# Cross-attention with a column-normalised softmax: a fused row minimum, a first batch by whole products, a last output in pieces, and new tables of order

## The chip, the cores and the metric

The kernel runs on one NeuronCore of a Trainium2 chip. The metric is the device time of one execution in microseconds (us), lower is better. The core has five engines that run side by side, each in its own program order: TensorE (PE in the profile, its weight loads PEld), VectorE (DVE), ScalarE (ACT), GpSimd (POOL) and SyncE (SP), which issues transfers. Matrix products are written to PSUM, eight banks of 512 fp32 columns on 128 partitions; everything else lies in SBUF.

## The reference

For each of 32 batches `x` and `y` (the input `ctx_2048`) are 256 x 1024 in fp32, and the three weights are 256 x 256.

```
x_q = (w_qk y)^T            x_k = w_qk x            x_v = w_v x + b_v
energy = x_q x_k                                      # 1024 x 1024
attention = softmax over the last axis of energy
attention = attention / (1e-7 + sum of attention over its rows)     # each column is normalised
x_r = x_v attention                                   # 256 x 1024
out = x + relu(w_t (x - x_r) + b_t)
```

## The kernel before

Algebra first. With G = w_qk^T w_qk, energy = y^T (G x), so each batch makes "keys" G x once and multiplies by y. The value path is folded: w_t w_v x is made directly ("values", `V`), and w_t x + b_t is made beside it (`x` products, `xP`). Energies carry a minus sign, so that a row **minimum** is what the softmax subtracts, and exp runs with scale -1.

Precision: each fp32 operand is split into a HIGH part and a LOW part of a faster fp32 form, and a product is three matmuls (HIGH HIGH, HIGH LOW, LOW HIGH, `ORDER`). A 2 x 2 block product is made by Winograd's scheme with seven block products instead of eight: `chain` (L278) makes the words P1 to P7 on three banks `a`, `b`, `c`; partial results are read out of `a` by ACT (`r1`, `r2`, `r3`) and added back by DVE (`c11`, `c22`, `c12`). Keys (`k`), energies (`E0` to `E3`) and x products (`x`) all go this way. So each `P` word is three matmuls of 512 columns on PE.

Energies are made in four pairs of row tiles, `E0` to `E3`. Tile n has 128 rows and 1024 columns and fills two banks: odd tiles banks 2 and 3 (`a` and `d`), even tiles banks 0 and 1 (`b` and `c`). The next pair's P1 writes bank `a` again, so it must wait until the odd tile of the pair before is read. The work of a tile is:

- the row minimum. Three of a pair's four blocks get theirs with the sum that makes them (`energy_block`, L451, on DVE with a running minimum). The fourth, the block `21` in bank `a`, is finished by PE itself, and `energy_least` (L463, the word `m21`) takes its minimum;
- `exp` on ACT with the minimum as bias and the row sum as second output, `ri` (reciprocal, DVE), `h` (ACT, exp times reciprocal, HIGH), `sum` (DVE, column sums into `acc`), `l` (DVE, LOW), for each half of 512 columns;
- `A n c h`: the attention product, three matmuls into one of banks 4 to 7.

After the last tile come `cols`, `inv`, `turn` (column sums, their inverse, spread over the partitions), `div` (DVE, banks 4 to 7 times the inverse into `z`), `join` (POOL, plus the x product), `pos` (ACT, relu), `add` (POOL, a transfer that adds x from memory) and `st` (SP, the store).

The order of everything is written out by hand in three tables of words, `FIRST`, `STEADY` and `LAST` (L575, L609, L629). A word with `+` belongs to the next batch, with `-` to the one before. Each engine gets its words in the order of the table and works them strictly in that order. The weights are prepared ahead of `FIRST`, in straight code: G, its seven left blocks in two parts (`left_blocks`, L173), w_t turned, w_v times w_t.

Of the kernel before, what the change touches and what calls it, by code (L numbers as in the profile page):

```python
# [17 lines left out]
def kernel(  # L18
# [142 lines left out]
    def gram(into, w):  # L161
        for k in range(KC):
            matmul(into[:, 0, :C], w[:, k, :P], w[:, k], k == 0, k == KC - 1)
            matmul(into[:, 1, P:C], w[:, k, P:], w[:, k, P:], k == 0, k == KC - 1)

    def square(into, left, right):
        for i in range(KC):
            for k in range(KC):
                matmul(
                    into[:, i, :C], left[:, k, ts(i, P)], right[:, k], k == 0, k == KC - 1  # L170
                )

    def left_blocks(name, to, w, engine):  # L173

        s = sums[name][:, 0].rearrange("p (s c) -> p s c", s=4)
        a11, a12, a21, a22 = (w[:, k, ts(i, P)] for i in range(2) for k in range(2))
        s1, s2, s3, s4 = (s[:, j] for j in range(4))
        engine.tensor_tensor(s1, a21, a22, ALU.add)
        engine.tensor_tensor(s3, a21, a11, ALU.subtract)
        engine.tensor_tensor(s2, s1, a11, ALU.subtract)  # L180
        engine.tensor_tensor(s4, a12, s2, ALU.subtract)
        act.copy(to[:, HIGH, 0:2], w[:, :, :P])
        act.copy(to[:, HIGH, 2], a22)
        act.copy(to[:, HIGH, 3:], s)
        engine.tensor_tensor(to[:, LOW, 0:2], w[:, :, :P], value(to[:, HIGH, 0:2]), ALU.subtract)
        engine.tensor_tensor(to[:, LOW, 2], a22, value(to[:, HIGH, 2]), ALU.subtract)
        engine.tensor_tensor(to[:, LOW, 3:], s, value(to[:, HIGH, 3:]), ALU.subtract)
# [384 lines left out]

    FIRST = """  # L575
        ldx0 ldx1 xT1 xh0 xl0 xT2 xh1 xl1 xT4 xTh1 xT3 xTl1 xTh0 xTl0 V00 V11 kP1 ldy0 kr1
        kP6 V10 kP5 ldy1 yh11 kr2 yh01 ys01 kP2 kP7 kr3 ys03 yh00 kc22 kc11 V01 kP3 kP4
        yl01 ys02 khD yl00 kc12 kT1 ys04 klD kh21 vh1 vh0 ysh0 kT3 vl1 kT2 kT4 kTh0 kl21
        kTh1 vl0 E0P2 +ldx0 ysl0 kTl1 xP1 E0P1 xP2 xP5 E0r1 yh10 xr1 E0P6 xP6 kTl0 E0r2
        +xh0 E0P7 E0c11 xc11 E0P5 E0r3 E0P4 E0c22 E0P3 E0m21 E0c12 exp1 +xT1 ys11 ys12 ri1  # L580
        sum10 ys14 h10 h11 l10 exp0 E1P1 E1r1 l11 A100 ri0 sum11 h01 +xl0 yl10 sum01 E1P6
        l01 E1r2 A111 sum00 E1P7 E1P5 yl11 h00 ys13 l00 E1r3 E1c22 E1P4 E1m21 xr2 E1P2
        +ldx1 ysh1 E1c11 E1P3 +xT3 E1c12 xP7 ysl1 exp3 ri3 sum30 xr3 h30 h31 exp2 l30 A000
        A011 xP4 xc22 l31 ri2 E2P1 xP3 E2r1 A311 sum31 E2P6 xc12 A101 h21 h20 E2r2 +xh1
        l21 E2P7 sum21 +xT2 sum20 l20 E2r3 xw21 E2P5 +ldy0 E2P4 E2c22 +yh01 +xTh0 E2m21
        E2P2 E2c11 E2P3 A110 A001 E2c12 exp5 ri5 sum50 +xl1 A211 A300 A301 h50 l50 exp4
        E3P1 h51 +xT4 E3r1 A010 ri4 +yh00 E3P6 sum51 A310 h41 E3r2 h40 E3P7 l51 sum41 l41
        sum40 E3r3 l40 E3P5 +xTh1 E3P4 E3c22 E3P2 A201 E3m21 +ldy1 E3P3 E3c11 +ys01 A200
        A210 exp7 A511 E3c12 +ys03 +yl01 ri7 h70 sum70 A510 +yh10 exp6 l70 +xTl0 +kP1
        +xTl1 sum71 ri6 +ys11 +yl00 +kr1 A501 +kP6 A410 h61 sum61 l61 +kr2 sum60 +kP7 h71  # L590
        +ys02 +ys13 +ys12 h60 l60 +ys04 +kP5 +kr3 A401 +kc22 +kP2 +ys14 l71 +kP3 +ysh0
        +kP4 +kc11 +khD +ysl0 +kc12 +kT1 +kh21 cols +kT2 +kl21 A710 +kT4 A701 A610 +kT3
        A500 A411 +klD A400 A711 +kTh1 +E0P1 +kTh0 +E0r1 inv turn +kTl1 A601 +kTl0 A700
        A611 +E0P6 A600 +E0P2 +E0r2 +yh11 +E0P7 div1 +E0P5 +E0r3 div0 ++ldx0 +E0P4 +ysh1
        +E0c22 +E0m21 +V10 +E0c11 +exp1 +ri1 +h10 +E0P3 +E0c12 +l10 +sum10 +exp0 +V11 +V01
        +ri0 +vh1 +E1P1 +h00 +sum11 +E1r1 +h11 +V00 +sum00 +h01 +E1P6 +vl1 +xP1 +l00 +E1r2
        +yl11 join0 +E1P7 +l11 +E1P2 +vh0 +l01 +E1r3 +sum01 +E1P5 +E1P4 +vl0 +E1c22 +xP2
        +xr1 pos0 ++xh0 join1 +ysl1 +xP6 +yl10 +E1P3 +E1m21 +E1c11 +E1c12 +exp3 ++ldx1
        +xP5 +A111 +xr2 +xP7 +ri3 +h30 +exp2 +xc11 +sum30 +xr3 +A100 +l30 +ri2 ++xT3 +A000
        +h20 +E2P1 +A300 +xP4 +sum31 ++xl0 +h21 +E2r1 +E2P6 +h31 +E2r2 ++xT1 +sum20 pos1  # L600
        +xc22 +l20 +l21 +xP3 +sum21 +E2P7 +xc12 +E2r3 ++xT2 +E2P5 +E2P4 ++ldy0 +l31 +E2P2
        +xw21 ++xh1 +E2c22 ++ys01 +E2P3 ++xT4 ++xTh0 +E2m21 +A110 +E2c11 +A101 +A010 +exp5
        +A011 +E2c12 +ri5 +sum50 +h50 +l50 +exp4 +A001 +ri4 +E3P1 +h40 ++xTl0 ++xl1 add1
        +E3r1 ++ys02 +h41 +h51 ++ldy1 +A200 +sum40 +A301 +l40 +E3P6 +l41 +sum51 +sum41
        +A311 +E3P2 +l51 ++ys04 ++yh00 +E3r2 ++ys03 +E3P7 ++yh01 +E3r3 +E3P5 ++xTh1 ++ys11
        +E3c11 st1 +A211 ++ysh0 +E3c22 +E3P4 +A310 +E3m21 +E3P3 ++yh11 +exp7 +E3c12 +ri7
        +sum70 +A500 +A210 +h70 +l70 +exp6 +A201 +A510 +sum71 +ri6 +h60 ++kP1
    """
    STEADY = """  # L609
        +xTl1 +yl01 +ys13 sum61 A400 A511 +kr1 h61 +kP6 +ysl0 +ys12 sum60 l60 +kr2 +kP2  # L610
        l61 +kP7 +kP5 A700 -add0 +yl00 +ys14 h71 +kr3 +kP4 cols +kc11 +kc22 +kP3 l71 A600
        +kc12 +khD +kT1 +kT3 A410 A501 A411 A710 A401 +kTh0 +kh21 +ysh1 +klD +kT2 +kTl0
        inv +kT4 +kl21 turn A711 A610 +kTh1 A611 A701 +E0P1 +E0P2 +E0r1 +kTl1 +yl11 +E0P6
        A601 +E0r2 +E0P7 -st0 +E0P5 div1 +E0c11 div0 +E0r3 +yh10 +E0c22 +E0P4 +E0P3 +E0m21
        +V10 +yl10 +V11 +E0c12 join1 +exp1 +ri1 +exp0 +V00 +h10 +sum10 +sum11 +ri0 +l10
# [62 lines left out]
```

## Time and profile before

| | |
|---|---|
| median of 3 runs | 2215.44 us (2185.95 to 2217.18) |
| the profiled execution | 2221.73 us, span of its instructions 2219.9 us |
| mean granted TensorE clock | 0.959 |
| busy PE / DVE / ACT / POOL | 1978.3 / 1718.9 / 1431.0 / 1401.6 us (89 / 77 / 64 / 63%) |
| transfers | 136.76 MB, mean 62 GB/s |

The profile is one execution. The span runs from the first to the last instruction, and the profiled execution's time is 1.8 us more. Engines overlap, so their busy times don't add. A row of a group of instructions gives the busy time and, behind it, the idle time of that engine just before them with what ended it. In the timeline a row's first number is the start, the second how long it took, and a bracket holds the idle time before it. Nearly all instructions are recorded under L62, a helper that keeps the order, so rows are told apart by tile names: `banks` is PSUM, `efs` the exponentials' HIGH and LOW parts, `small` the per-row numbers, `acc` the column sums, `rs` the read-out blocks, `gf` keys, `yd` and `ysum` the parts of y, `xf` those of x, `uf` and `vws` values, `gws` and `tws` the left blocks of weights, `z` and `xe` the output and the x product. The fused sum with a running minimum is CUSTOM_DVE_ANT_0 in the profile, followed by a DVE_READ_ACCUMULATOR2_ANT that delivers the minimum.

### The profile page before, as it was taken

How to read it: one execution, taken by the hardware profiler on the slowest of the kernel's cores; microseconds unless marked ns; L12 is line 12 of the kernel's file. 1: busy time of each engine (PE TensorE's matmuls, PEld its weight loads, DVE VectorE, ACT ScalarE, POOL GpSimd, SP SyncE). 2: the span in 40 equal slices, each digit the busy share in tenths (PEclk: the TensorE clock that was granted, in tenths of full speed). 3: DMA queues.
4: the chain of work that ended last, by engine and by line, in shares of the span. 5: the costliest groups of instructions: out<-in, count | busy, mean ns of one | idle time of the engine just before them, and what ended most of it. 6: DMA issues, size and time to landing. Idle time of an engine off the chain costs nothing. (4 is left out here: it accounts for less than half of the span.)

```text
span 2219.9 us, 25140 instructions
## 1 busy us (share of the span) xinstructions
PE 1978.3 (89%) x8671; PEld 1552.5 (70%) x8671; DVE 1718.9 (77%) x3049; ACT 1431.0 (64%) x2227; POOL 1401.6 (63%) x974
## 2 busy tenths in 40 slices
PE   6898989889898889898899988898989998988986
PEld 4677777777777777676777766776777777767775
DVE  2787877778778787777787777877877877878875
ACT  4676666766667666666666666666766666666663
POOL 7476666566666656766667656567667667566661
PEclk8999999999999999999999999999999999999998
DMA  1112212212122122122221221212221212212213
GB/s 64 39 49 76 67 48 67 76 48 67 48 76 67 48 76 60 55 67 57 68 67 48 76 67 48 76 49 65 67 76 49 75 49 68 67 51 74 67 29 76
DMA packets 46432, 136.76 MB, mean 62 GB/s; under 512 B 4448, under 2 KB 5344, under 8 KB 46304
## 3 DMA queue, kind: packets, MB, share of 16 engines
q1 hardware_dynamic: 36672, 101.20, 12.8%
q0 software_dynamic: 9216, 33.56, 9.1%
q8 instruction: 68, 1.11, 0.2%
q14 instruction: 60, 0.49, 0.1%
q10 hardware_dynamic: 416, 0.39, 0.1%
HBM read 101.58 MB, written 33.55 MB: 61 GB/s over the span
## 5 line engine op out<-in xcount | busy, mean ns | idle before, releaser
L62 PE MATMUL banks<-efs,uf 128*128 128x512 f32 x3072 | 801.6, 401 | 1.3 <-DVE efs L62 1.3
L62 PEld LDWEIGHTS banks<-efs,uf 128*128 128x128 f32 x3072 | 597.4, 195 | 134.1 <-DVE efs L62 2.2
L62 PE MATMUL banks<-gf,yd 128*128 128x512 f32 x1152 | 347.5, 421 | 184.3 <-ACT efs L62 144.7
L62 ACT COPY rs<-banks 128x512 f32<-128x512 f32 x480 | 283.0, 590 | 265.4 <-PE banks L62 264.9
L62 DVE SCALAR_TENSOR_TENSOR acc<-banks,small,acc 128x512 f32<-128x512 f32 x448 | 334.8, 747 | 142.7 <-ACT efs L62 139.3
L62 PE MATMUL banks<-gf,ysum 128*128 128x512 f32 x1536 | 442.6, 407 | 1.5 <-DVE acc L62 0.3
L62 ACT ACTIVATE banks<-banks,small 128x1024 f32<-128x1024 f32 x256 | 278.0, 1086 | 246.9 <-DVE small L62 246.8
L62 ACT ACTIVATE efs<-banks,small 128x512 fp32r<-128x512 f32 x512 | 350.0, 692 | 114.0 <-DVE small L62 108.0
L62 PEld LDWEIGHTS banks<-gf,yd 128*128 128x128 f32 x1152 | 210.8, 195 | 278.4 <-ACT efs L62 83.0
L62 DVE SCALAR_TENSOR_TENSOR efs<-banks,small,efs 128x512 fp32r<-128x512 f32 x512 | 369.7, 743 | 17.3 <-ACT efs L62 17.2
L62 PEld LDWEIGHTS banks<-gf,ysum 128*128 128x128 f32 x1536 | 283.9, 193 | 110.3 <-ACT rs L62 42.5
L62 POOL TENSOR_TENSOR gf<-sums,gf 128x1024 fp32r<-128x1024 f32 x96 | 229.4, 2404 | 177.5 <-ACT gf L62 177.5
L62 POOL TENSOR_TENSOR sums<-raws 128x256 f32<-128x256 f32 (+1 forms) x192 | 185.2, 966 | 159.6 <-DMA raws<-in_ctx_dram 152.0
L62 POOL TENSOR_TENSOR xf<-raws,xf 128x1024 fp32r<-128x1024 f32 x64 | 153.4, 2397 | 175.2 <-ACT xf L62 166.0
L62 POOL TENSOR_TENSOR xf<-sums,xf 128x1024 fp32r<-128x1024 f32 x64 | 153.1, 2394 | 156.4 <-ACT xf L62 156.4
L62 PEld LDWEIGHTS banks<-vws,xf 128*128 128x128 f32 x1536 | 210.4, 206 | 19.8 <-ACT xf L62 8.5
L62 PE MATMUL banks<-vws,xf 128*128 128x256 f32 x1536 | 211.1, 297 | 10.9 <-ACT xf L62 7.5
L62 DVE CUSTOM_DVE_ANT_0 banks<-banks,rs 128x512 f32<-128x512 f32 x256 | 176.5, 694 | 48.5 <-PE banks L62 35.5
L62 PE MATMUL banks<-xf,gws 128*128 128x512 f32 x672 | 180.6, 405 | 21.7 <-ACT yd L62 14.5
L62 PE MATMUL banks<-xf,tws 128*128 128x512 f32 x672 | 190.6, 392 | 3.0 <-ACT rs L62 2.9
L62 POOL TENSOR_TENSOR yd<-raws,yd 128x512 fp32r<-128x512 f32 (+1 forms) x128 | 138.1, 1079 | 70.8 <-ACT yd L62 70.7
L62 PEld LDWEIGHTS banks<-xf,gws 128*128 128x128 f32 x672 | 118.7, 188 | 72.7 <-ACT banks L62 30.9
(76 smaller groups left out, 2380.7 us busy)
## 6 DMA issues: line engine op xcount, KB each, us to landing
raws<-in_x_dram SPq DMA_DIRECT2D x64, 512.0 KB, 4.2
raws<-in_ctx_dram SPq DMA_DIRECT2D x64, 512.0 KB, 4.0
z<-in_x_dram POOLq DMA_DIRECT2D x64, 512.0 KB, 5.3
out_dram<-z SPq DMA_DIRECT2D x64, 512.0 KB, 3.2
z<-in_L_xattn_w_t_dram ACTq DMA_DIRECT2D x1, 256.0 KB, 4.8
z<-in_L_xattn_w_v_dram SPq DMA_DIRECT2D x1, 256.0 KB, 5.9
z<-in_L_xattn_w_qk_dram ACTq DMA_DIRECT2D x1, 128.0 KB, 2.7
z<-in_L_xattn_w_qk_dram SPq DMA_DIRECT2D x1, 128.0 KB, 2.5
```

Of the source, the lines that this page charges most:

```text
L62: self.last = getattr(self.engine, name)(*args, **kwargs)
```

## The change

Four parts.

1. `energy_least` is one fused instruction instead of two: it adds zeros to the block in bank `a`, writes it back in place, and takes the running minimum from `mB`.
2. The first batch does without Winograd's scheme for its keys (`first_keys`, 24 matmuls for 21), its x products (`first_x`, 24 for 21) and its first pair of tiles (`first_energy`, 24 for 21). So the weights' seven left blocks aren't needed at the start; their making (words `G...` and `T...`) goes into `FIRST` and moves to POOL. x's HIGH and LOW parts of the first batch are partly made on DVE (`Fxh0`, `Fxl0`, `Fxl1`). y's first half is loaded at the start.
3. The last batch's output isn't divided, joined, rectified, added to by a transfer and stored by 1024 columns, but in halves: with relu(d + e) + x written as max(d, -e) + (x + e), `Zs` makes x + e and `Zn` -e ahead of time, and after the last attention products there remain `Zd` (divide in place, in PSUM), `Zm` (maximum), `Za` (sum) and `Zt` (store).
4. `FIRST`, `STEADY` and `LAST` are new tables; `STEADY` now begins at `E0P1`, and the last two batches are in `LAST`.

```diff
     def energy_least(b, p):
-        dve.tensor_reduce(small["mD", b, p], eb["a"], AX.X, ALU.min)
-        dve.tensor_tensor(small["m1", b, p], small["mD", b, p], small["mB", b, p], ALU.min)
+        dve.tensor_tensor_reduce(
+            out=eb["a"],
+            in0=eb["a"],
+            in1=zeros_row,
+            scale=1.0,
+            scalar=small["mB", b, p],
+            op0=ALU.add,
+            op1=ALU.min,
+            accum_out=small["m1", b, p],
+        )
...
+    zeros_row = nc.const_aps.tensor(0.0, [P, MB], F32)
...
+    def first_keys(j, m, k):
+        for i in range(KC):
+            for h in range(MH):
+                matmul(
+                    (kb["b"], kb["c"], kb["a"], banks[:, 3])[2 * i + h],
+                    gt[:, j, k, ts(i, P)],
+                    xf[:, m, 2 * k + h],
+                    (j, m, k) == (HIGH, HIGH, 0),
+                    (j, m, k) == (LOW, HIGH, 1),
+                )
+    def whole(into, left, right):
+        for j, m in ORDER:
+            for k in range(KC):
+                matmul(
+                    into, left(j, k), right(m, k),
+                    (j, m) == ORDER[0] and k == 0, (j, m) == ORDER[-1] and k == KC - 1,
+                )
...
+    def xl_dve(k):
+        at = slice(2 * k, 2 * k + 2)
+        dve.tensor_tensor(
+            flat(xf[:, LOW, at]), raws["x", 0, k], flat(value(xf[:, HIGH, at])), ALU.subtract
+        )
...
+    def first_least(b, n):
+        dve.tensor_reduce(small[f"m{n}", b, 0], flat(tile_banks(n)), AX.X, ALU.min)
...
+    def out_divided(b, c, h):
+        p = pair(2 + c)[:, h]
+        dve.scalar_tensor_tensor(p, p, ubias[:, c], rc[:, ts(h, MB)], ALU.add, ALU.mult)
+    def out_max(b, c, h, kept):
+        p = pair(2 + c)[:, h]
+        dve.tensor_tensor(p if kept else z[:, c, ts(h, MB)], p, xe[:, c, ts(h, MB)], ALU.max)
+    def out_add(b, c, h, kept):
+        zh, o = z[:, c, ts(h, MB)], raws["o", b, c][:, ts(h, MB)]
+        if kept:
+            dve.tensor_tensor(zh, pair(2 + c)[:, h], o, ALU.add)
+        else:
+            pool.tensor_tensor(zh, zh, o, ALU.add)
...
     STEADY = """
-        +xTl1 +yl01 +ys13 sum61 A400 A511 +kr1 h61 +kP6 +ysl0 +ys12 sum60 l60 +kr2 +kP2
...
+        E0P1 -cols ysh1 kTh1 -inv --st0 kTl1 -A610 -A601 -A711 E0r1 kTh0 -turn E0P6 -div0
...
-    for b in range(1, B - 1):
+    for b in range(1, B - 2):
         do(STEADY, b)
```

How the tables move instructions, at three places.

DVE, where a batch's first energy pair begins, in every steady batch. Before, from the turned inverse (STREAM_TRANSPOSE, `turn`) on: the second row is `div1`, the next two `E0c11`, then `div0`, `E0c22`, `E0m21` (two rows) and `E0c12`. ISA is the fused sum and, on 128x1, its accumulator's read.

```order
L62 STREAM_TRANSPOSE acc<-sc 128x1024
L62 SCALAR_TENSOR_TENSOR z<-banks,ubias,acc 128x1024
L62 ISA banks,small<-banks,rs 128x512
L62 ISA small 128x1
L62 SCALAR_TENSOR_TENSOR z<-banks,ubias,acc 128x1024
L62 ISA banks,small<-banks,rs 128x512
L62 ISA small 128x1
L62 TENSOR_REDUCE small<-banks 128x1
L62 TENSOR_TENSOR small<-small 128x1
L62 ISA banks,small<-banks,rs,small 128x512
```

The same place on DVE in the changed kernel: `turn`, `div0` and `div1`, `E0c22`, the new `E0m21`, `E0c11`, `ri1`, `E0c12`.

```order
L62 STREAM_TRANSPOSE acc<-sc 128x1024
L62 SCALAR_TENSOR_TENSOR z<-banks,ubias,acc 128x1024 x2
L62 ISA banks,small<-banks,rs 128x512
L62 ISA small 128x1
L62 ISA banks,small<-banks,const-float32-0.0,small 128x512
L62 ISA small 128x1
L62 ISA banks,small<-banks,rs 128x512
L62 ISA small 128x1
L62 RECIPROCAL small<-small 128x1
L62 ISA banks,small<-banks,rs,small 128x512
```

Both divisions now stand ahead of `E0c22`, `E0c11` stands behind the minimum, and the reciprocal of the odd tile stands ahead of `E0c12`.

PE in the same batch, from the third pair's last products to the fourth pair's first. Before, from `E2P4 E2P2` (two words, six matmuls on `gf,yd`): three attention words, `E2P3`, one attention word, then `E3P1`.

```order
L62 MATMUL banks<-gf,yd 128x512 x6
L62 MATMUL banks<-efs,uf 128x512 x9
L62 MATMUL banks<-gf,ysum 128x512 x3
L62 MATMUL banks<-efs,uf 128x512 x3
L62 MATMUL banks<-gf,yd 128x512 x3
```

In the changed kernel, from `E2P4` on: `E2P3`, five attention words, `E3P1`.

```order
L62 MATMUL banks<-gf,yd 128x512 x3
L62 MATMUL banks<-gf,ysum 128x512 x3
L62 MATMUL banks<-efs,uf 128x512 x15
L62 MATMUL banks<-gf,yd 128x512 x3
L62 MATMUL banks<-efs,uf 128x512 x6
```

Between the product that finishes the odd tile's block (`E2P4`) and the one that overwrites its bank (`E3P1`) stood six words, `E2P2` among them; `E2P2` has moved ahead, and there stand six.

PE at the start of the program. With - the values' and keys' products of before, with + those of the changed kernel: the turned w_t (`z`, 128x128), G's corner, w_v times w_t (128x256), the 24 key products and the 48 value products.

```order
-L62 MATMUL banks<-xe,z 128x256 x4
-L62 MATMUL banks<-vws,xf 128x256 x24
-L62 MATMUL banks<-xf,gws 128x512 x6
-L62 MATMUL banks<-vws,xf 128x256 x12
+L62 MATMUL banks<-z 128x128 x5
+L62 MATMUL banks<-z,rs 128x128
+L62 MATMUL banks<-z 128x256 x4
+L62 MATMUL banks<-xf,efs 128x512 x24
+L62 MATMUL banks<-vws,xf 128x256 x48
```

The keys now stand ahead of all values, and read x's two parts alone, not the sums of x's blocks that POOL makes.

More of the change, by code (lines that the diff above doesn't have):

```diff
@@ L159, in load_y, with word, once @@
         )
[L161 to L187, printed above, removed]
+    words = {}
+    def word(name, do, *args):
+        words[name] = lambda b: do(b, *args)
+    def once(name, do, *args, **more):
+        words[name] = lambda b: do(*args, **more)
     for k, start in enumerate((load, act.dma_start)):
@@ L571 @@
         word(f"st{c}", stored, c)
-    FIRST = """
[L576 to L607, printed above, removed]
@@ L608 @@
     """
     STEADY = """
-        +xTl1 +yl01 +ys13 sum61 A400 A511 +kr1 h61 +kP6 +ysl0 +ys12 sum60 l60 +kr2 +kP2
[L611 to L615, printed above, removed]
@@ new lines @@
+        E0r2 E0P2 --st1 +ldx0 -A611 kTl0 E0P7 -div1 E0r3 E0P5 E0c22 E0P4 yl10 E0m21 E0c11
+        V11 exp1 ri1 E0P3 h10 -join0 ysl1 V10 V00 h11 E0c12 exp0 sum10 l10 sum11 ri0 vh1
+        sum01 E1P1 E1r1 h00 V01 h01 vl1 E1P6 E1r2 xP1 E1P7 vh0 +ldx1 l00 l01 sum00 l11
+        E1r3 xr1 +xh0 E1P5 E1P2 E1P4 vl0 E1c22 A111 E1m21 exp3 xP2 xP6 E1c11 E1P3 -join1
+        xc11 xr2 xP5 ri3 xP7 A011 A100 E1c12 h30 sum30 l30 exp2 sum31 ri2 E2P1 xr3 xP4
+        +xT3 xc22 h20 +xT1 E2r1 xP3 sum20 h21 l20 E2P6 h31 E2P2 A000 +xl0 +xT2 E2r2 xw21
@@ new lines @@
+        --A611 -E0P6 --A610 --turn -E0r2 -E0P2 --div0 -E0P7 -E0r3 --div1 -ysl1 -E0P5
+        -E0c22 -E0P4 -E0m21 -E0c11 -V11 -exp1 -E0P3 ldx0 --join1 -yl10 -ri1 -h10 -h11 -V10
+        -E0c12 -sum10 -l10 -V01 -E1P1 -exp0 -vh1 -E1r1 ldx1 -V00 -sum11 -l11 -ri0 -h01
+        -h00 -E1P6 -vl1 -sum00 -l00 -l01 -E1r2 -sum01 -vh0 -xP1 -E1P7 -vl0 -E1P5 -xr1
+        -E1r3 -E1P4 xh0 -E1c22 -E1P2 -E1m21 -exp3 -E1P3 -xP6 -E1c11 xT1 -xr2 -E1c12
+        --join0 -ri3 -h30 -sum30 -exp2 -l30 -A111 -xP5 -xP2 -xP7 -E2P1 -xc11 -xr3 -ri2
@@ L636, in do @@
+        Zt00 Za01 Zt11 Zt01
+    """
+    done = {(name, 0) for name in "ldx0 ldx1 ldy0 kP1 kP2 kP3 kP4 kP5 kP6 kP7 kr1 kr2 kr3 kc11 kc22 kc12 khD klD xP1 xP2 xP3 xP4 xP5 xP6 xP7 xr1 xr2 xr3 xc11 xc22 xc12 xw21 xT1 xT2 xT3 xT4 xTh0 xTh1 xTl0 xTl1 E0P1 E0P2 E0P3 E0P4 E0P5 E0P6 E0P7 E0r1 E0r2 E0r3 E0c11 E0c22 E0c12 E0m21 xh0 xl0 xl1".split()}
+    done |= {(name, B - 1) for name in "div0 div1 join0 join1 pos0 pos1 add0 add1 st0 st1".split()}
     def do(text, b):
```

259 lines of the change are left out of this document (211 added, 48 removed).

## The prediction

> **What bounds the kernel now.** I read the page's first part for the engines, then where batches begin, then two batches side by side, then the waits of PE, then the timeline around the longest of them. The column sums `cols` run once a batch, on DVE; the view of their tile gives the first and last start.
>
> ```profile
> PE 1978.3 (89%) x8671; PEld 1552.5 (70%) x8671; DVE 1718.9 (77%) x3049; ACT 1431.0 (64%) x2227; POOL 1401.6 (63%) x974
> L62 DVE TRANSPOSE_TENSOR_REDUCE parts<-acc x32: 1234/1237/1240, 108.9 to 2196.6; 128x32 f32<-128x1024 f32 x32
> ```
>
> So 108.9 us go by before the first `cols`, 31 batch periods take 2087.7 us (67.35 each), and 23.3 us of the 2219.9 follow the last. The periods are not alike. Two neighbours, from the view by stretches (length, then busy PE, PEld, DVE, ACT, POOL, the granted clock):
>
> ```profile
> 1593.27:1662.05 68.78, 62.02 (x271) 48.88 (x271) 54.03 (x96) 44.58 (x70) 43.58 (x30) 0.95 0.22 62
> 1662.05:1726.37 64.32, 59.27 (x271) 46.51 (x271) 51.70 (x97) 44.22 (x70) 43.64 (x30) 1.00 0.24 66
> ```
>
> The same 271 matmuls take 64.3 us at full clock and 68.8 us at 0.95. PE is idle 5.0 and 6.8 us of it, no other engine comes near its length. PE bounds, with waits, and the clock goes with the waits. Stretches of 3.41 us, each followed by the next:
>
> ```profile
> 1480.40:1483.81 3.41, 1.48 (x13) 1.28 (x11) 1.90 (x5) 1.80 (x4) 3.41 (x3) 0.99 0.00 0
> 1483.81:1487.23 3.42, 2.88 (x10) 2.62 (x11) 3.25 (x5) 3.20 (x5) 1.22 (x1) 0.51 0.01 2
> 2019.70:2023.11 3.41, 1.53 (x13) 1.32 (x11) 1.86 (x5) 1.80 (x5) 3.41 (x3) 1.00 0.00 0
> 2023.11:2026.53 3.42, 2.84 (x18) 2.65 (x19) 3.25 (x5) 3.42 (x6) 1.25 (x2) 1.00 0.03 7
> ```
>
> With PE busy 1.48 us of such a stretch the next ran at half clock, with 1.53 at full. A wait of some 1.9 us within one stretch therefore costs a second time. What PE waits for, from 180 to 2140 us (total, times, longest), with the wait of `exp` behind it:
>
> ```profile
> ACT banks L62 <- DVE small L62: 224.0, 116, 3.2
> PE banks L62 <- ACT efs L62: 142.2, 58, 2.9
> PE banks L62 <- DVE efs L62: 26.7, 57, 0.6
> ```
>
> Two long waits a batch, 2.45 us each, before `E1P1` and `E3P1`, and some of 0.6. The first, in the fast batch (the row at 1677.61 is `E0P4`, which finishes bank `a`; behind it PE does `E0P3` and three value words):
>
> ```profile
> 1677.61 0.96 PE L62 MATMUL banks<-gf,yd 128*128 128x512 f32 x3
> 1678.53 0.96 PE L62 MATMUL banks<-gf,ysum 128*128 128x512 f32 x3
> 1678.61 0.69 DVE L62 TENSOR_REDUCE small<-banks 128x1 f32<-128x512 f32 x1
> 1678.63 2.40 POOL L62 TENSOR_TENSOR z<-z,xe 128x1024 f32<-128x1024 f32 x1
> 1679.33 1.72 DVE L62 TENSOR_TENSOR small<-small 128x1 f32<-128x1 f32 x1
> 1679.33 4.46 PE L62 MATMUL banks<-vws,xf 128*128 128x256 f32 x36
> 1681.08 1.09 ACT L62 ACTIVATE banks<-banks,small 128x1024 f32<-128x1024 f32 x1 [3.23 <-DVE small L62]
> 1686.27 0.93 PE L62 MATMUL banks<-gf,yd 128*128 128x512 f32 x3 [2.48 <-ACT efs L62]
> ```
>
> The minimum of two numbers per row (1679.33) takes 1.72 us and ends at 1681.05, when POOL's instruction ends (1681.03). In the slow neighbour the same before `E3P1`: DVE from 1638.01 for 2.29 to 1640.30, POOL to 1640.28.
>
> ```profile
> 1637.88 2.40 POOL L62 TENSOR_TENSOR xf<-raws,xf 128x1024 fp32r<-128x1024 f32 x1
> 1638.01 2.29 DVE L62 TENSOR_TENSOR small<-small 128x1 f32<-128x1 f32 x1
> 1644.10 1.53 PE L62 MATMUL banks<-gf,yd 128*128 128x512 f32 x3 [2.78 <-ACT efs L62]
> ```
>
> **Part 1, the fused minimum, and the new order around it.** The rows by shape, of the two that go, of the fused sum with a running minimum that comes, and its accumulator's read:
>
> ```profile
> L62 DVE TENSOR_TENSOR small<-small 128x1 f32<-128x1 f32 x128 | 138.7, 1083 | 4.4
> L62 DVE CUSTOM_DVE_ANT_0 banks<-banks,rs,small 128x512 f32<-128x512 f32 x128 | 96.2, 751 | 5.1
> L62 DVE TENSOR_REDUCE small<-banks 128x1 f32<-128x512 f32 x128 | 88.3, 690 | 26.6 <-PE banks L62 22.0
> L62 DVE DVE_READ_ACCUMULATOR2_ANT small<- 128x1 f32 x384 | 53.7, 140 | 0.0
> ```
>
> Per minimum 0.69 + 1.08 = 1.77 us go and 0.75 + 0.14 = 0.89 come: DVE saves 0.88 us, four times a batch, 3.5 us of 54. That alone is no time, since DVE isn't the bound; what counts is `exp`, earlier by 0.88 on average and by 1.6 where POOL held it. The fused form reads one operand in PSUM and one in SBUF, like the 128 of its row (mean 751 ns, no long ones), so I take no hold by POOL; they also write their sums into a bank, so the writing back costs nothing extra.
>
> What is late next, by the new tables. From the finished block on: `exp` 0.9 us later (0.75 + 0.14), and from `exp` to the free bank, where nothing else stands between, these rows of the third pair in the fast batch:
>
> ```profile
> 1705.74 1.09 ACT L62 ACTIVATE banks<-banks,small 128x1024 f32<-128x1024 f32 x1 [0.94 <-DVE small L62]
> 1708.63 0.74 DVE L62 SCALAR_TENSOR_TENSOR efs<-banks,small,efs 128x512 fp32r<-128x512 f32 x1
> 1709.52 0.93 PE L62 MATMUL banks<-gf,yd 128*128 128x512 f32 x3 [0.66 <-ACT efs L62]
> ```
>
> 3.8 us from `exp` to the next pair's P1, so 4.7 from the end of P4 to P1. PE covers it with words of 0.68 us (in the rows below nine attention matmuls take 2.04 us from start to the next word's start, 0.227 each) and value words of 1.4 to 1.5:
> - `E1P1`: behind `E0P4` stand a value word, `E0P3` and two value words. That is some 5 us, the cover it had; what shrinks is the chain (`h10` no longer stands behind the other tile's `exp`, 1.1 us, and the hold of 1.6 is gone). Wait 2.48 becomes 0.1.
> - `E2P1`: nine words, 5.3 us from P4's end. Wait 0.6 becomes 0.2, since `vl0` and `E1c22` hold the minimum for half a us.
> - `E3P1` and the next `kP1`: six words, 3.9 us. Waits of 2.4 and 0.6 become 0.8 to 1.1 and 0.8.
>
> ```profile
> 1705.30 2.20 PE L62 MATMUL banks<-efs,uf 128*128 128x512 f32 x9
> 1707.34 0.84 PE L62 MATMUL banks<-gf,ysum 128*128 128x512 f32 x3
> ```
>
> About 2.0 us of waits, none near 1.9 in one piece, so no half clock by the stretches above. The rest I hold at the fast batch's 59.3 us of busy PE: 61.3 us a batch. From below, words at their dense spacing (74 of 0.68 and 4 of 1.42) make 56.0, and 58 with the waits; from above it is today's fast batch, 64.3. New stalls speak for more: ACT now does a second `h` and a y cast between `kr2` and `kr3`, neither longer than the 1.09 us of an `exp`, which may hold `kP3` for about 1 us. Others go (0.6 before `E3P2` among those of PE on DVE). I take **61.4**: 31 x (67.35 - 61.4) = **184 us**. DVE then is at 50.2 of 61.4, and both divisions stand ahead of `E0c22` and `E0m21`. `div1` needs `A611`, which ends three words, 2.1 us, before `E0P4` does; a division of 1.28 (below) and `E0c22` of 0.75 just fit in. That is the tightest place, and I count no wait there.
>
> **Part 2, the start.** The first `exp` starts at 55.27 now, and PE gives 34.6 us of work to it:
>
> ```profile
> 0.00:55.30 55.30, 34.56 (x133) 26.33 (x133) 14.74 (x26) 23.90 (x43) 41.43 (x39) 0.81 0.19 64
> 8.86 3.47 PE L62 MATMUL banks<-xe,z 128*128 128x256 f32 x8 [1.55 <-ACT xe L62]
> 19.44 0.58 PE L62 MATMUL banks<-vws,xf 128*128 128x256 f32 x1 [7.12 <-ACT xf L62]
> ```
>
> After w_v times w_t (ended 12.3) PE now waits 7.1 us, and POOL is busy 41.4 of 55.3. Changed: keys 24 x 0.227 = 5.4 us, values 48 x 0.124 = 6.0 (36 in 4.46 above), tiles 5.4, together 16.8 at full clock and 20.7 at this stretch's 0.81, after 12.3; key read-outs that nothing covers some 4 x 0.69, the minimum of 1024 columns at most 2 x 0.69. `exp` at 37: 18 us earlier. At half clock it is 53, a gain of 2; with full clock 22. The 9 matmuls more are 2 us, in the sum already. The left blocks on POOL lie beside the first batch's tiles.
>
> The Trainium skill, "Advanced Engine Details and Errata", GPSIMD Details under Miscellaneous Facts, says POOL shares an interface with DVE and conflicts with DVE instructions of two SBUF inputs or in a two-port mode. The two holds quoted above agree, and by it the change brings three such instructions in: `Fxh0`, `Fxl0`, `Fxl1`. Each could be held for one POOL instruction of up to 2.40 us, and the start's gain would be as little as 11 instead of 18.
>
> **Part 3, the end.**
>
> ```profile
> 2201.07 2.79 PE L62 MATMUL banks<-efs,uf 128*128 128x512 f32 x11 [1.34 <-DVE efs L62]
> 2203.90 1.28 DVE L62 SCALAR_TENSOR_TENSOR z<-banks,ubias,acc 128x1024 f32<-128x1024 f32 x1 [0.35 <-PE banks L62]
> 2208.31 1.06 ACT L62 ACTIVATE z<-z 128x1024 f32<-128x1024 f32 x1 [1.25 <-POOL z L62]
> 2209.66 0.86 POOL L62 DMA_DIRECT2D z<-in_x_dram  x1 [0.58 <-ACT z L62]
> 2213.72 2.90 SPq L561 DMA_DIRECT2D out_dram<-z  x2
> out_dram<-z SPq DMA_DIRECT2D x64, 512.0 KB, 3.2
> ```
>
> From PE's end (2203.86) to the span's end 16.0 us. Changed: behind it stand two divisions, two maxima and a sum on DVE, 5 x 0.7 = 3.5 (512 columns, as in the rows by shape), and a store, issue included at most the 3.2 of twice the size: 6.7. **Gain 9**, 7 to 11.
>
> **The sum.** 2221.7 - 184 - 18 - 9 = **2010 us** for the profiled execution's kind. That execution is 6 us over the median, within its share of half-clock stretches, which I expect gone; so I don't subtract the 6 again.
>
> **Rivals.**
> - *Other waits take the place.* What `exp` gives back is lost at `kP3`, at the two divisions or at POOL (`kT2` now ahead of `klD`), and a batch stays at today's fast 64.3: 31 x 2.9 = 90 us more than forecast, 2105. For it: chains within 0.5 us of their cover at four places. Against: POOL idles 20 us a batch.
> - *Denser still.* The stutters of 0.1 to 0.4 us around the block read-outs go too, 59.4 a batch: 1948.
> - *The fused minimum is held too*, because zeros are read from SBUF. Then 0.9 us come back on each chain, waits reach 1.9 and half clock stays: about 67 a batch, 2185. The 128 rows of 751 ns speak against.
> - *Slower.* `E0c22` and the minimum stand behind both divisions. Were DVE late there, each us late is a us of every batch, as PE has nothing left ahead of `E1P1`. It decides from 6.6 us late (205 us over 31), and 9 a batch would make 2290. DVE has 50 us of work in 61, so I see no such backlog.
>
> **How the numbers follow.** Forecast (60.2 to 62.8 a batch) 0.60, other waits 0.17, denser 0.13, held 0.05, slower 0.05. The range 1950 to 2105 takes in the first three and the bounds of start and end. A measurement of this kernel tells 2% (44 us) from no change; below 2171 lie the first three and a little, 0.90; within 2% 0.06; above 0.04.
>
> **What would show it.** In the profile after: no 128x1 TENSOR_TENSOR on `small`; a fused row with zeros of 0.75 us, 127 times; `cols` 61.4 us apart; a granted clock of 0.98 or more between 100 and 1900; PE's waits for `efs` under 70 us in total, none over 1.5; the first `exp` before 40; 14 us from the last `cols` to the end. It would be wrong if the waits for `exp` stay, if PE waits behind `z` or `gf` instead, or if half clock stays in most batches.

## The result, and the profile after

The changed kernel takes **1973.6 us** (median of four), where the kernel before took 2208.5 beside it: ratio 0.895, 95% interval 0.886 to 0.904. Three of the four executions took 1973.3 to 1973.7; the fourth took 9255.2 at full clock, for which the record shows no reason. Forecast were 2010, in a range of 1950 to 2105. The profiled execution spans 1971.5 us.

The page of the changed kernel, its busy times and the granted clock in 40 slices, then the first and last start of `cols`:

```profile
PE 1893.3 (96%) x8680; PEld 1495.7 (76%) x8680; DVE 1606.0 (81%) x3044; ACT 1430.9 (73%) x2223; POOL 1395.1 (71%) x975
PEclk9999999999999999999999999999999999999999
L62 DVE TRANSPOSE_TENSOR_REDUCE parts<-acc x32: 1235/1236/1239, 74.5 to 1955.2; 128x32 f32<-128x1024 f32 x32
```

A 9 stands for nine tenths or more; the mean granted clock of this execution is 0.999 (before 0.959). The same cut as before gives three parts:

| us | before | after | difference | forecast |
|---|---|---|---|---|
| up to the first `cols` | 108.9 | 74.5 | -34.4 | -18 |
| 31 batch periods | 2087.7 | 1880.7 | -207.0 | -184 |
| after the last `cols` | 23.3 | 16.3 | -7.0 | -9 |

All three have the forecast sign; the start and the batches gained more. Two steady batches after (length, then busy PE, PEld, DVE, ACT, POOL, the granted clock):

```profile
804.99:865.90 60.91, 58.73 (x271) 46.52 (x270) 50.02 (x96) 44.64 (x69) 43.69 (x31) 1.00 0.25 70
865.90:926.87 60.97, 58.77 (x271) 46.50 (x270) 49.99 (x96) 44.66 (x69) 43.61 (x31) 1.00 0.25 69
```

Both are alike: 60.9 and 61.0 us, PE idle for 2.2 of it, no half clock. DVE has 50.0 us in it, as the prediction had (50.2). The engines' waits, from 180 to 1900 us (total, times, longest), and the new minimum among the groups by shape:

```profile
ACT banks L62 <- DVE small L62: 97.4, 111, 1.9
ACT efs L62 <- DVE acc L62: 62.4, 58, 1.7
PE banks L62 <- DVE efs L62: 35.8, 58, 0.6
PE banks L62 <- ACT rs L62: 23.7, 29, 0.9
L62 DVE CUSTOM_DVE_ANT_0 banks<-banks,const-float32-0.0,small x127: 758/759/761, 35.9 to 1949.2; 128x512 f32<-128x512 f32 x127
```

The two long waits are gone: PE's row for ACT's `efs` (142.2 us before) no longer stands among the waits, and no wait of PE in this stretch is over 0.9. All 127 fused minima take 758 to 761 ns; none is held. What PE still waits for is 0.63 us before `E3P1`, 0.63 before the next `kP1` (both in the row for DVE's `efs`), and a new one of 0.86 before `E3P7`, in the row for `rs`. The timeline shows where that comes from (`sum51`, `sum41` on DVE, `h41` and the read-out `E3r2` on ACT, `E3P7` on PE):

```profile
905.19 1.40 DVE L62 SCALAR_TENSOR_TENSOR acc<-banks,small,acc 128x512 f32<-128x512 f32 x2
906.62 0.69 ACT L62 ACTIVATE efs<-banks,small 128x512 fp32r<-128x512 f32 x1 [1.07 <-DVE acc L62]
907.21 0.58 ACT L62 COPY rs<-banks 128x512 f32<-128x512 f32 x1
907.84 1.43 PE L62 MATMUL banks<-gf,ysum 128*128 128x512 f32 x5 [0.88 <-ACT rs L62]
```

`h41` reads the same bank as `sum41`, which the new table puts first; ACT waits 1.07 us for it, the read-out stands behind, and PE behind the read-out.

### The profile page after: what moved, and what is told of

It is laid out like the page before. It is cut to its first block, busy times and chain, and to the rows that moved or that the text cites. A ratio compares the mean times of both kernels' runs of the same rounds, so it can differ in the third digit from the quotient of the medians.

```text
span 1971.5 us, 25233 instructions
## 1 busy us (share of the span) xinstructions
PE 1893.3 (96%) x8680; PEld 1495.7 (76%) x8680; DVE 1606.0 (81%) x3044; ACT 1430.9 (73%) x2223; POOL 1395.1 (71%) x975
## 5 line engine op out<-in xcount | busy, mean ns | idle before, releaser
L62 PE MATMUL banks<-efs,uf 128*128 128x512 f32 x3072 | 780.5, 390 | 0.0
L62 PEld LDWEIGHTS banks<-efs,uf 128*128 128x128 f32 x3072 | 576.7, 188 | 124.2
L62 PE MATMUL banks<-gf,ysum 128*128 128x512 f32 x1524 | 421.1, 398 | 26.8 <-ACT rs L62 25.8
L62 ACT ACTIVATE efs<-banks,small 128x512 fp32r<-128x512 f32 x512 | 340.3, 693 | 122.5 <-DVE acc L62 68.2
L62 ACT COPY rs<-banks 128x512 f32<-128x512 f32 (+1 forms) x475 | 278.0, 585 | 188.2 <-PE banks L62 175.6
L62 PE MATMUL banks<-gf,yd 128*128 128x512 f32 x1158 | 333.8, 400 | 23.3 <-DVE efs L62 20.0
L62 PE MATMUL banks<-xf,gws 128*128 128x512 f32 x651 | 195.3, 417 | 19.8 <-DVE efs L62 19.7
L62 PEld LDWEIGHTS banks<-vws,xf 128*128 128x128 f32 x1536 | 196.3, 190 | 8.2
L62 DVE CUSTOM_DVE_ANT_0 banks<-banks,rs 128x512 f32<-128x512 f32 x254 | 179.0, 705 | 22.2 <-PE banks L62 16.9
L62 PE MATMUL banks<-xf,tws 128*128 128x512 f32 x651 | 168.3, 389 | 0.0
L62 POOL TENSOR_TENSOR ysum<-sums,ysum 128x1024 fp32r<-128x1024 f32 x64 | 158.7, 2480 | 8.2 <-ACT ysum L62 8.2
L62 ACT CAST gf<-sums 128x1024 fp32r<-128x1024 f32 x95 | 99.9, 1053 | 76.1 <-DVE sums L62 76.0
```

What stands on the lines that cost most here:

```text
L62: self.last = getattr(self.engine, name)(*args, **kwargs)
```

## Experiments

Theory A, the prediction's: the minimum of two numbers was held while POOL ran, because it reads two SBUF operands; without it the chain from P4 over `exp` to the next P1 is short, and the half clock goes with the waits. Rivals: B, the new tables alone do it; C, what counts is DVE's saved work, or the hold has another cause than the two operands; D, half clock costs nothing. Ratios are against the kernel before, timed beside each run at medians of 2218 to 2223 us.

### 1. The fused minimum alone

```diff
-        dve.tensor_reduce(small["mD", b, p], eb["a"], AX.X, ALU.min)
-        dve.tensor_tensor(small["m1", b, p], small["mD", b, p], small["mB", b, p], ALU.min)
+        dve.tensor_tensor_reduce(out=eb["a"], in0=eb["a"], in1=zeros_row, scale=1.0,
+            scalar=small["mB", b, p], op0=ALU.add, op1=ALU.min, accum_out=small["m1", b, p])
```

> The kernel before with only the fused minimum put in (old tables, old start, old end). If the two-step minimum is what makes the long chains: the wait before E1P1 falls from 2.47 to about 0.9 us and the one before E3P1 likewise, no half clock is left in the batches, a batch is about 62.8 us instead of 67.35, and the time is about 2075 us. If the new tables alone made the gain, or if only the 3.5 us of VectorE work a batch count, which is not the bound: 2190 to 2215, no difference.

Measured: **2056.1 us**, ratio 0.926 (0.923 to 0.930). PE's waits in this kernel, from 180 to 2140 us, and one batch by stretches:

```profile
PE banks L62 <- ACT efs L62: 42.2, 58, 1.2
PE banks L62 <- DVE efs L62: 38.2, 68, 1.4
968.90:1031.36 62.46, 59.40 (x271) 46.55 (x271) 49.87 (x96) 44.20 (x70) 43.69 (x30) 1.00 0.25 68
```

PE's wait for ACT's `efs` (what `h` makes of `exp`'s result) fell from 142.2 us to 42.2, the longest from 2.9 to 1.2; a batch is 62.46 us at full clock, 62.8 was expected. The total is 19 us under the expected 2075, 7.5 of them because the first `cols` comes at 101.4 instead of 108.9. B falls: 7.4% of the time goes, of the 10.5% of the whole change, by this one line with old tables, old start and old end. The first half of C falls too, since DVE is idle for 12.6 of the batch's 62.46 us: its work isn't the bound.

### 2. The two steps, with one SBUF operand each

```diff
+    duo = Ring("duo", 12, [2])
...
-            accum_out=small[least, b, p],
+            accum_out=duo[b, p][:, 1:] if least == "mB" else small[least, b, p],
...
-        dve.tensor_reduce(small["mD", b, p], eb["a"], AX.X, ALU.min)
-        dve.tensor_tensor(small["m1", b, p], small["mD", b, p], small["mB", b, p], ALU.min)
+        dve.tensor_reduce(duo[b, p][:, :1], eb["a"], AX.X, ALU.min)
+        dve.tensor_reduce(small["m1", b, p], duo[b, p], AX.X, ALU.min)
```

> The kernel before with the same two steps for the minimum, but the second is a reduction over the two neighbouring numbers of a [128,2] tile instead of a minimum of two separate operands: one SBUF input instead of two, the same count of instructions, the same tables. If the second step was held because it reads two SBUF operands while POOL works: it takes about 0.2 us every time, a batch is about 62.9 us without half clock, and the time is about 2080 us. If any short VectorE instruction on SBUF was held beside POOL, or the hold had another cause (a semaphore, the bank): the second step still shows 1.5 to 2.4 us at E1 and E3, and the time stays at 2190 to 2215.

Measured: **2052.4 us**, ratio 0.925 (0.922 to 0.927), as much as by the fused form. The second step, by shape:

```profile
L62 DVE TENSOR_REDUCE small<-duo 128x1 f32<-128x2 f32 x128 | 19.9, 155 | 4.4
```

155 ns in the mean (154 to 160), where the form with two operands took 1083, with as many instructions, at the same places, beside the same POOL work. The operation differs too, a reduction instead of a TENSOR_TENSOR, but that isn't it: in the kernel before, the 96 TENSOR_TENSORs `xe<-banks,rs`, with one operand in PSUM and one in SBUF, took 671 to 694 ns each, and the 64 of `uf<-banks,uf` 1211 to 1226, so none was held. So it is the two SBUF operands, and C falls. The Trainium skill, "GPSIMD Engine Reference", section Key points, says that GpSimd shares its SBUF interfaces with VectorE and contends with DVE instructions of two SBUF inputs. By that rule the step with one input is free and the one with two isn't; this run agrees.

### 3. Only the half clock taken away

```diff
+                if at >= 2 and name in ("E1P1", "E3P1"):
+                    into = pair(2)[:, 1, :C] if name == "E1P1" else pair(2)[:, 0, :C]
+                    for _ in range(3):
+                        matmul(into, zeros, zeros_half, name == "E1P1", True)
```

> The kernel before with three fp32 matmuls of zeros, 128x128 by 128x256, in PE's program just ahead of E1P1 and again ahead of E3P1, from the third batch on: they add nothing to the result and fill some of PE's wait there, which by itself stays as long. If a short stretch without matmuls costs a second time, by half clock in the next 3.41 us: the granted clock is 0.99 or more in the batches, a batch is 64.4 to 65 us instead of 67.35, and the time is 2110 to 2150 us, though PE has more work. If half clock costs nothing, or has another cause than PE's idling: the clock stays at 0.96 and the time at 2200 to 2230.

Measured: **2170.2 us**, ratio 0.978 (0.974 to 0.981), with a granted clock of 0.990 over the whole execution (0.959 before) and no half clock in the batches. The place before `E1P1` (zeros, then `E1P1`), and a batch:

```profile
1111.08 1.47 PE L62 MATMUL banks<-const-float32-0.0 128*128 128x256 f32 x6
1113.73 0.93 PE L62 MATMUL banks<-gf,yd 128*128 128x512 f32 x3 [1.19 <-ACT efs L62]
1089.53:1155.75 66.22, 61.91 (x283) 48.63 (x283) 53.63 (x96) 44.19 (x70) 43.61 (x30) 1.00 0.23 64
```

1.47 us of zeros and 1.19 of idling stand where 2.48 of idling stood: the chain is about as long as before, the gap in one piece is half, and the time falls by 53 us, clear of the spread of either kernel's runs, although PE has 2.9 us of zeros a batch more to do. D falls. The time is 20 us above the range that I expected, since I had taken a batch of 64.3, which has only one of the two long waits; with both (59.3 busy and 6.8 idle, the slow neighbour's) it makes 66.1, as measured. The half clock's own share is thus some 53 us, and the waits' some 114 (2170 less 2056).

### 4. The new tables with the old minimum

```diff
-        dve.tensor_tensor_reduce(out=eb["a"], in0=eb["a"], in1=zeros_row, scale=1.0,
-            scalar=small["mB", b, p], op0=ALU.add, op1=ALU.min, accum_out=small["m1", b, p])
+        dve.tensor_reduce(small["mD", b, p], eb["a"], AX.X, ALU.min)
+        dve.tensor_tensor(small["m1", b, p], small["mD", b, p], small["mB", b, p], ALU.min)
```

> The changed kernel with only the old two-step minimum put back. If the two-step minimum is what makes the long chains (the 128x1 step held until POOL's running instruction ends): the 128x1 rows are again above 0.9 us in the mean, with single ones of 1.5 to 2.4 us, PE's waits for exp's results grow by 0.9 us or more at two or three places of a batch, a batch is 65 to 67 us instead of 60.95, and the time is 2100 to 2160 us. If the new tables alone made the gain: PE covers the longer chains, a batch stays near 61.5, and the time is 1975 to 2000.

Measured: **2339 us** as the median of 2283, 2338, 2340 and 2358, each slower than the kernel before, by 3 to 6%, and outside both expectations. B falls once more: without the new minimum the new tables lose. A is right in kind only: the step was held, but much longer than by one POOL instruction. From the profiled execution (2338 us) the row by shape, then the fourth pair's minimum and all of POOL beside it:

```profile
L62 DVE TENSOR_TENSOR small<-small 128x1 f32<-128x1 f32 x127 | 329.9, 2598 | 4.3
...
1085.40 7.00 DVE L62 TENSOR_TENSOR small<-small 128x1 f32<-128x1 f32 x1
...
1084.23 2.57 POOL L62 TENSOR_TENSOR xf<-sums,xf 128x1024 fp32r<-128x1024 f32 x1
1086.60 2.14 POOL L62 TENSOR_TENSOR yd<-raws,yd 128x512 fp32r<-128x512 f32 x2
1088.54 0.88 POOL L62 TENSOR_TENSOR sums<-sums,raws 128x256 f32<-128x256 f32 x1
1089.22 2.48 POOL L62 TENSOR_TENSOR ysum<-sums,ysum 128x1024 fp32r<-128x1024 f32 x1
1091.52 0.86 POOL L62 TENSOR_TENSOR sums<-raws 128x256 f32<-128x256 f32 x1
...
1096.25 1.65 PE L62 MATMUL banks<-xf,gws 128*128 128x512 f32 x3 [7.53 <-DVE efs L62]
```

The minimum begins under `xTl1` (1084.23), which ends at 1086.80, and it isn't let in there: POOL's next instruction begins at once, and so four more times, until at 1092.38 POOL has none ready. The minimum ends at 1092.40, and PE starts `kP1` at 1096.25 after a wait of 7.5 us. In 22 of the 32 batches this step takes 6.9 to 7.0 us. In seven others it takes 1.26 to 1.34, for instance:

```profile
1905.30 2.41 POOL L62 TENSOR_TENSOR xf<-sums,xf 128x1024 fp32r<-128x1024 f32 x1
1906.48 1.26 DVE L62 TENSOR_TENSOR small<-small 128x1 f32<-128x1 f32 x1
1907.66 1.99 POOL L62 TENSOR_TENSOR yd<-raws,yd 128x512 fp32r<-128x512 f32 x2
```

Here the minimum gets in as `xTl1` ends (1907.71), although POOL's next instruction follows just as promptly. So a ready successor alone doesn't keep it out. In the 22 batches the successor is recorded from 0.15 to 0.24 us ahead of `xTl1`'s end, in the seven 0.05 to 0.13; whether that decides it, no run here shows. Of all 127 two-operand steps the 123 that took over 0.3 us end 14 to 30 ns behind the end of a POOL instruction.

### 5. The same, with POOL made to pause

```diff
         dve.tensor_tensor(small["m1", b, p], small["mD", b, p], small["mB", b, p], ALU.min)
+        if p == 3:
+            pool.tensor_copy(paused, small["m1", b, p])
```

> The changed kernel with the old two-step minimum (2339 us), and behind the fourth pair's minimum a copy of its result on GpSimd, so that GpSimd's next instruction waits until VectorE has the minimum. In the old-minimum run that step took 7.0 us in most batches, through five further GpSimd instructions, and 1.34 in some. If it is passed over each time GpSimd goes straight to its next instruction: with the pause it takes 1.2 to 1.4 us in every batch, the wait before kP1 falls from 6.4 to about 0.7, a batch is 66 to 68.3 us instead of 74.9, and the time is 2090 to 2150 us, although GpSimd has an instruction and a wait more a batch. If the 7 us have another cause than the GpSimd instructions that follow: the step stays at 7 and the time at 2280 to 2350.

Measured: **2190.8 us**, ratio 0.989 (0.986 to 0.992), 92 us under the quickest run without the pause and 148 under their median, by one more instruction on POOL. The place in this kernel:

```profile
1013.24 2.57 POOL L62 TENSOR_TENSOR xf<-sums,xf 128x1024 fp32r<-128x1024 f32 x1
1014.43 1.41 DVE L62 TENSOR_TENSOR small<-small 128x1 f32<-128x1 f32 x1
1015.91 0.18 POOL L62 COPY paused<-small 128x1 f32<-128x1 f32 x1
...
PE banks L62 <- DVE efs L62: 129.9, 77, 1.8
```

The fourth pair's minimum now takes 1.41 us and ends with `xTl1`, in each steady batch (1.39 to 1.43). So it was POOL's following instructions that had kept it out in the 22 batches. A batch is 67 to 68.2 us, as expected; the total isn't, because I had added it up wrongly (31 batches of 67.3 with 84.2 ahead and 16.7 behind are 2188), and `kP1` waits 1.8 us instead of 0.7: its minimum takes 0.69 + 1.41 us where the fused one takes 0.76 + 0.14, 1.2 more than in the changed kernel, where `kP1` waits 0.63. The other three minima are held as before (some 1.2, 1.8 and 2.2 us), and PE waits 1.7 us before `E1P1` and before `E3P1`.

### 6. Two steps without the second operand, in the new tables

```diff
-            accum_out=small[least, b, p],
+            accum_out=duo[b, p][:, 1:] if least == "mB" else small[least, b, p],
...
-        dve.tensor_tensor_reduce(out=eb["a"], in0=eb["a"], in1=zeros_row, scale=1.0,
-            scalar=small["mB", b, p], op0=ALU.add, op1=ALU.min, accum_out=small["m1", b, p])
+        dve.tensor_reduce(duo[b, p][:, :1], eb["a"], AX.X, ALU.min)
+        dve.tensor_reduce(small["m1", b, p], duo[b, p], AX.X, ALU.min)
```

> The changed kernel with the fused minimum replaced by two reductions, the second over the two neighbouring numbers of a [128,2] tile: two steps as in the kernel before, but one SBUF input each. If all that the fused form brings is that no short step with two SBUF operands is held beside GpSimd: 0.69 + 0.16 us against 0.75 + 0.14, no difference, 1965 to 1980 us. If the saving of an instruction, or the fused form itself, matters in the new tables: nearer to 2000 or to the 2339 of the new tables with the old minimum.

Measured: **1976.4 us**, ratio 0.891 (0.889 to 0.893), as the first expectation had it. The fused form itself brings nothing to be seen beyond the operand that it saves (1973.6 beside 1976.4).

### 7. The start, with the keys late

```diff
     def xh_dve(k):
+        for _ in range(8):
+            dve.tensor_copy(raws["x", 0, k], raws["x", 0, k])
```

> The changed kernel with eight copies of the first half of the first x onto itself on VectorE, ahead of the HIGH part that the first keys read: TensorE stands idle for some 2 to 6 us between w_v times w_t and the keys. Let d be how much later the first key product starts than the 8.62 us of the changed kernel. If the start came out 16 us better than my sum because no half clock was left there: the stretch of 3.41 us behind the idle one runs at half clock, as before, and the first exp comes later than 25.61 by d plus 1.7 us or more. If the clock at the start has nothing to do with such a gap: full clock throughout, and the first exp later by d or less. The total follows by the same amount, 1973.6 plus 4 to 9 us in the first case.

Measured: **1981.1 us**, 7.5 more than the changed kernel. The keys on PE, the first `exp`, and two stretches:

```profile
13.14 7.26 PE L62 MATMUL banks<-xf,efs 128*128 128x512 f32 x24 [3.70 <-DVE xf L62]
31.58 1.09 ACT L62 ACTIVATE banks<-banks,small 128x1024 f32<-128x1024 f32 x1 [0.94 <-DVE small L62]
10.24:13.65 3.41, 0.51 (x1) 0.50 (x2) 3.34 (x5) 0.03 (x1) 3.33 (x4) 0.91 0.00 0
13.65:17.07 3.42, 3.42 (x11) 2.53 (x10) 2.90 (x3) 3.33 (x7) 3.42 (x3) 0.59 0.31 78
```

d is 13.14 - 8.62 = 4.5 us, and `exp` comes 31.58 - 25.61 = 6.0 later: 1.45 us more than the delay. The 24 keys take 7.26 us instead of 5.82, and the clock is 0.91 and 0.59 in the two stretches. That is less than the 1.7 expected, but more than the delay alone, and the half clock is there. So a gap of this kind at the start costs the clock; the changed kernel has none, and its clock is 1.00 up to the first `exp`. The Trainium skill, "TensorE: Matmul & The Clock Gate", section "Why this matters for your kernels", asks for no idle gap of more than about 3 us; the gap of 3.70 here agrees, while in the kernel before some 1.9 us of idling in a stretch of 3.41 (PE busy for 1.48) were already followed by half clock, and there the measurement decides.

### 8. `h` ahead of the sum, and one word more

The wait before `E3P7` points to an order of words. In `STEADY`, on top of the changed kernel:

```diff
-        E2P3 -pos1 A110 E2c12 exp5 A311 ri5 A010 A001 sum50 h50 exp4 A300 l50 +yh00 E3P1
+        E2P3 -pos1 A110 E2c12 exp5 A311 ri5 A010 A001 h50 sum50 exp4 A300 l50 +yh00 E3P1
...
-        +ldy1 A310 E3P6 sum41 h51 h41 E3P2 E3r2 -pos0 E3P7 l41 E3r3 E3P5 +xTh1 E3c11 l51
+        +ldy1 A310 E3P6 h51 h41 sum41 E3P2 E3r2 -pos0 E3P7 l41 E3r3 E3P5 +xTh1 E3c11 l51
...
-        A200 A301 A410 sum70 h70 exp6 l70 sum71 ri6 +kP1 +kr1 A201 sum61 sum60 h61 +yh01
+        A200 A301 A410 h70 sum70 exp6 l70 sum71 ri6 +kP1 +kr1 A201 sum61 sum60 h61 +yh01
```

> The changed kernel with three pairs of words in STEADY exchanged: h50 ahead of sum50, h51 and h41 ahead of sum41, h70 ahead of sum70, so that ScalarE's h doesn't wait about 1.07 us for VectorE's sum on the same bank. If the wait of 0.86 us before E3P7 comes from h41 standing ahead of the read-out E3r2 on ScalarE: it falls to about 0.1, the waits before E3P1 and the next kP1 from 0.63 to about 0.4, and 28 batches by 1.1 us give about 1943 us. If the sum, read later, then delays l and the free bank by as much: the same total, about 1973.

Measured: **1942.1 us** (1941.8 to 1942.2), ratio 0.876 (0.874 to 0.878). The waits from 180 to 1900 us, and a batch:

```profile
ACT efs L62 <- DVE acc L62: 3.8, 4, 1.7
PE banks L62 <- DVE efs L62: 16.1, 30, 1.0
PE banks L62 <- DVE small L62: 15.5, 27, 0.6
PE banks L62 <- ACT rs L62: 0.6, 2, 0.3
911.49:971.34 59.85, 58.69 (x271) 46.58 (x270) 49.73 (x97) 44.74 (x69) 43.61 (x31) 1.00 0.26 71
```

PE's waits for read-outs fell from 23.7 us to 0.6, those of ACT for the sum from 62.4 to 3.8, a batch from 60.95 to 59.85, as expected; `E3P1` and `kP1` still wait 0.57 and 0.52, where 0.4 was expected. This beats both kernels, by 31 us the changed one.

Then the attention word `A211` moved ahead of `E3P1`:

```diff
-        E2P3 -pos1 A110 E2c12 exp5 A311 ri5 A010 A001 h50 sum50 exp4 A300 l50 +yh00 E3P1
-        A211 +ys03 +xT4 +xl1 +ys01 ri4 +ys02 +xTl0 +ys04 -add1 sum51 h40 E3r1 l40 sum40
+        E2P3 -pos1 A110 E2c12 exp5 A311 ri5 A010 A001 h50 sum50 exp4 A300 l50 +yh00 A211
+        E3P1 +ys03 +xT4 +xl1 +ys01 ri4 +ys02 +xTl0 +ys04 -add1 sum51 h40 E3r1 l40 sum40
```

> The version with h ahead of the sum (1942.1 us), and the attention word A211 moved ahead of E3P1 on TensorE. If the wait of 0.57 us before E3P1 is a chain that one word more (0.68 us) covers, and the read-out E3r1 behind it is covered by A310 alone: 28 batches by 0.5 us, 1927 to 1930. If the read-out then isn't covered: the wait moves to E3P6, and the time stays at 1940 to 1944.

Measured: **1938.3 us** (1937.9 to 1938.5), ratio 0.875 (0.871 to 0.879). The wait went, 15.5 us to 0.2 in that row:

```profile
PE banks L62 <- DVE small L62: 0.2, 1, 0.2
```

The gain is 3.8 us and not the 12 to 15 of the first expectation, and the wait didn't move to `E3P6` as in the second, which had 1940 to 1944. Per batch 0.6 us of idling are saved, yet the batch is only 0.12 shorter: from a word's start to the next it now takes 0.11 to 0.16 us more at `A310`, `E3P6`, `E3P7` and `E3P5`, in pieces too short to be listed as PE's waits. So most of what the wait had cost was spread over the words behind it, and not won; by what, no run here shows.

## Why the prediction was right, and where it was off

**The mechanism.** Right, and shown: the hold by POOL for two SBUF operands (experiments 1, 2, 5, 6), the short chain as what counts (a batch of 62.5 us with 50 of DVE in it, experiment 1, isn't bound by DVE), the half clock that goes with the waits (3). The prediction took the hold to last as long as one POOL instruction, and that is true of the kernel before, where the longest step took 2.44 us; in the new tables it can last through six (4). The fused form isn't held (758 to 761 ns), so that rival is out. The *slower* rival (both divisions ahead of `E0c22`) didn't come: PE doesn't wait before `E1P1` at all.

**The batches, 184 forecast, 207 measured.** A steady batch is 60.95 where I took 61.4. The terms: `E1P1` 0.1 forecast, 0 measured; `E2P1` 0.2 and 0; `E3P1` 0.8 to 1.1 and 0.63; the next `kP1` 0.8 and 0.63; `kP3` about 1, no wait of PE. The 0.86 before `E3P7` I didn't see; it took `kP3`'s place by chance. The idle sum of 2.2 is thus close to 2.0 in part by luck, by other terms, and busy PE is 58.75 instead of 59.3. A batch is 0.45 us shorter than forecast, which makes 14 of the 23 us. The other 9 are the last two periods, 56.9 and 56.5 us: they prepare fewer batches to come, and I had counted all 31 alike.

Of the 6.7 us a batch, the fused minimum with old tables gives 5.1 (62.2 in the mean of experiment 1's 31), the new tables 1.5. But the parts don't add: with the old minimum the new tables, start and end together are 3 to 6% slower than the kernel before. My sum didn't say that the tables rest on the minimum.

**The start, 18 forecast, 34 measured: the term that was mis-sized most.** The rows of the changed kernel (w_v times w_t, keys, values, the first `exp`):

```profile
6.98 1.99 PE L62 MATMUL banks<-z 128*128 128x256 f32 x8 [0.57 <-ACT z L62]
8.62 5.82 PE L62 MATMUL banks<-xf,efs 128*128 128x512 f32 x24
14.28 5.92 PE L62 MATMUL banks<-vws,xf 128*128 128x256 f32 x48
25.61 1.09 ACT L62 ACTIVATE banks<-banks,small 128x1024 f32<-128x1024 f32 x1 [0.93 <-DVE small L62]
```

I had `exp` at 37; it starts at 25.6. w_v times w_t ends at 8.97, not at 12.3 as before (3.3 us). From the keys' start to the tiles' end it is 16.9 us, the 16.8 of the sum at full clock; I had divided them by the old stretch's 0.81, and experiment 7 shows that such a clock comes with a gap and not with the start as such (3.9). And 4.2 us of read-outs and minimum that I had laid bare are covered: the 48 value products stand between keys and tiles, and the odd tile's minimum ends while PE finishes the even one. That makes 11.4. A further 4.7 came between the first `exp` and the first `cols`, which I hadn't counted as the start.

The three DVE instructions of the start took 0.69, 1.22 and 1.39 us. One of POOL's beside the last shows the price on the other side:

```profile
10.85 0.74 POOL L62 TENSOR_TENSOR sums<-sums,xe 128x256 f32<-128x256 f32 x1
11.27 1.39 DVE L62 TENSOR_TENSOR xf<-raws,xf 128x1024 fp32r<-128x1024 f32 x1
11.66 1.60 POOL L62 TENSOR_TENSOR sums<-xe,sums 128x256 f32<-128x256 f32 x1
```

POOL's second takes 1.60 where the first of the same shape took 0.74, while DVE runs its subtraction with two SBUF operands; PE waited for neither. So the lower gain of 11 that the prediction put beside its 18 didn't come.

**The end, 9 forecast, 7 measured.** PE's last products, the last divisions, the stores:

```profile
1950.31 14.44 PE L62 MATMUL banks<-efs,uf 128*128 128x512 f32 x63
1964.11 1.44 DVE L62 SCALAR_TENSOR_TENSOR banks<-banks,ubias,acc 128x512 f32<-128x512 f32 x2 [0.18 <-PE banks L62]
1964.78 3.53 SPq L756 DMA_DIRECT2D out_dram<-z  x4
```

From PE's end (1964.75) to the span's end it is 6.75 us, forecast 6.7, before 16.0. So this term gained 9.3 where it was meant; measured from the last `cols` it is 7.0, since `cols` now stands elsewhere among the last products.

**Figures that don't come out of their own terms.** Three beside the sum, none of which moves it: the start at half clock is 12.3 + 33.6 + 4.1 = 50 and not 53; 90 us more than the forecast is 2100 and not 2105; and before `E2P1` stand eight words, whose 5.3 us are right, and not nine.

## What to carry to other kernels

Look for the smallest instructions on a critical chain, not only for the costly groups: a 128x1 step with two SBUF operands, 0.16 us by itself, took up to 7 us beside a busy GpSimd, and the same result from one operand took 0.16 every time. Compare such an instruction's end with the other engine's ends; where they agree to a few hundredths of a us, it was held. And a part that alone is worth 7% may be what the rest stands on: with the old step the new order was slower than the old one, so undo parts one by one before crediting the order.

## What the runs showed of the hardware that I had not expected

A held VectorE instruction isn't always let in at the next end of a GpSimd instruction: in 22 of 32 batches it was passed over five times (7.0 us instead of some 1.3), and one wait on GpSimd ended that (1.41 in every steady batch). That GpSimd's next instruction stands ready isn't enough for it, since in seven batches it did and the step got in at once; what decides stays open. The hold goes both ways: a GpSimd instruction of 0.74 us took 1.60 in the one place seen, beside a VectorE one with two SBUF operands. And filling 1.47 of a 2.5 us gap with matmuls of zeros was worth 2.2% of the kernel's time by the clock alone.
